# Linear attention and MoE on one core: first pair of q among k's last steps, written order from k's last quarter on

## The chip, the cores and the metric

The kernel runs on one core of a Trainium2 chip. The metric is the device time of one execution in microseconds (us); lower is better. The engines are TensorE (PE; its weight loads are PEld), VectorE (DVE), ScalarE (ACT), GpSimd (POOL) and SyncE (SP), which here only issues transfers (DMAs). GpSimd issues transfers of its own.

## The reference

`x` has 2048 tokens of 512 channels, all numbers are float32. First comes a layer norm and linear attention with 32 heads of 64, then a layer norm and a mixture of 8 experts of which each token takes two:

```python
h = layernorm(x)
q, k, v = relu(h @ Wq), relu(h @ Wk), h @ Wv          # (2048, 512) @ (512, 2048)
kv = einsum('hsd,hse->hde', k, v); key_sum = k.sum(tokens)
out = (q @ kv) / clip(q . key_sum, 1e-6)               # for each head
x = x + out @ Wo + bo
f = layernorm(x)
top2 = top_k(f @ gate_w.T + gate_b + bias, 2); gates = softmax(top2)
x = x + sum over the two experts: gate * (silu(f @ w1[e].T + b1[e]) @ w2[e].T + b2[e])
```

## The kernel before

**Numbers.** A float32 operand is split into a high and a low part (`split`: a cast on ScalarE, a subtraction on VectorE or GpSimd), and a product is three products of parts (`mm3`, L175 to L177). So each weight that is loaded (`raw_load` into one of four `raw` buffers) costs a cast and a subtraction (`raw_split`, L181) before TensorE can use it.

**Steps of k and g.** The inner width of 2048 is worked in four quarters `j` of 512, the tokens in 16 tiles `t` of 128. A step is `s = 16 j + t`; there are 64. `a_step(s)` loads what the next step needs, splits weights that fall due, multiplies the tile with Wk (`a_k`: products `pk`, then relu on ScalarE at L298, low part and running sum on VectorE at L299 and L307), and multiplies the normed tokens of step `s - 1` with that step's k (`a_g`: four banks `g`, summed over the quarter). Because v is linear in the tokens, kv follows from g and Wv once a quarter: `a_kv(j - 1)` at the third step of the next quarter, with the key sums `pks` (L355). In the first quarter each step also normalises and transposes a tile (`a_norm`), and writes it to DRAM (`xnd`), from where later quarters load it (`a_xn`).

**Work laid beside the steps.** w1 of the experts is split and written back to DRAM in 22 pieces, one a step from step 16 to 37 (one staging buffer, `stage`). k's next weights are loaded at `t == 8` and split at 9 to 12, v's loaded at 12 and split at 13 and 14. GpSimd fills rows of `out` and of the routed tokens `xs_d` with zeros (31 and 7 transfers, early in the kernel), copies part of Wq and w2 in DRAM, adds sums of token halves (`a_sums`, for the pairs below), and stores the transposed tokens to DRAM (`xtd`, in steps 32 to 47).

**Pairs of q.** The first two quarters of q are computed for pairs of token tiles with seven products instead of eight (Strassen's scheme in Winograd's form): `group(i)` for eight pairs. A group makes `p1, p6, p7, p4, p5, p2, p3` (`b_p`), adds them up on VectorE into four q's, normalises each (`normalised`, L444 to L449: five VectorE operations), and turns and multiplies the four q's of the pair before (`b_t`: four transposes, a cast, a subtraction; `b_o2`: 12 triples of products). The weights of the seven products lie where k's tokens were (`w7`), so tokens must be loaded back (`reload`, from `xtd`) for the last two quarters of q. Those run tile by tile (`b_q`, `b_n`, `b_t`, `b_o`, `b_add`), as do the routing and the experts after them.

**Wo.** `b_w(j, p)` splits a part of Wo, `b_m(j, p)` multiplies it with kv into `m_at` (`pm`), so that the output is q times m.

**What sets the order.** Outside of `with tc.manual_schedule(engines=...)` a scheduler orders each engine's instructions by its own estimate of time; inside of it, the named engines take them as written. Before, the 64 steps are ordered by the scheduler, with `hold(held, behind)` as the only order given by hand; groups are in written order on all engines but GpSimd (L1111), the steps 34 to 47 of q by the scheduler again, what follows by hand. Each engine takes its instructions in order, and so do the queues of SyncE and GpSimd.

Of the kernel before, what the change touches and what calls it, by code (L numbers as in the profile page):

```python
# [26 lines left out]
def linear_attention__then__moe_kernel(  # L27
# [207 lines left out]
    def norm(xt, dst):  # L235
        sm = const.tile([P, 16], FP, tag="sm", bufs=3, name="sm")
        st, mv, sd, rs = sm[:, 0:6], sm[:, 6:8], sm[:, 8:9], sm[:, 9:10]
        first = nc.vector.bn_stats(st, xt)
        nc.vector.bn_aggr(mv, st)
        root = nc.scalar.activation(sd, mv[:, 1:2], AF.Sqrt, bias=eps)  # L240
        nc.vector.reciprocal(rs, sd)
        last = nc.vector.tensor_scalar(dst, xt, mv[:, 0:1], rs, ALU.subtract, ALU.mult)
        return first, root, last
# [18 lines left out]
    def transpose4(src, name):  # L262
        tp = aux_bank(name)
        tp3 = tp.rearrange("p (c s) -> p c s", c=4)
        for c in range(4):
            nc.tensor.transpose(tp3[:, c, :], src[:, ts(c, P)], ident)  # L266
        return tp3
# [4 lines left out]
    def a_norm(t):  # L272
        xn = fpb.tile([P, C], FP, tag="xn", bufs=3, name="xn")
        ins = norm(xs.pop(t), xn)
# [54 lines left out]
    def a_kv(j):  # L329

        for p0 in range(0, PP, 2):
            pkv = aux_bank("pkv").rearrange("p (a l b) -> p a l b", a=2, l=2)
            for p in range(p0, p0 + 2):
                for c in range(CC):
                    w, g = slot_n[0][:, c], g_at(j)[:, c]
                    nc.tensor.matmul(
                        pkv[:, p - p0], w[:, 0, ts(p, P)], g[:, :, ts(p, P)],
                        start=c == 0, stop=False,
                    )
                    nc.tensor.matmul(  # L340
                        pkv[:, p - p0, 0, :], w[:, 1, ts(p, P)], g[:, 0, ts(p, P)],
                        start=False, stop=c == CC - 1,
                    )
            for r in range(0, P, D):
                o = slice(r, r + D)
                kv = fpb.tile([P, 2, D], FP, tag="kvs", bufs=2, name="kvs")[o]
                nc.scalar.copy(kv, pkv[o, :, 1, o])
                nc.vector.tensor_add(kv, kv, pkv[o, :, 0, o])
                split(kvt[o, 0, p0 : p0 + 2, o], kvt[o, 1, p0 : p0 + 2, o], kv)
        words(nc.sync, kvd[j], kvt)  # L350
        pks = aux_bank("pks")
        ka = frw.tile([P, 2, QW], FR, tag="xs", bufs=3, name="ka")
        split(ka[:, 0, :], ka[:, 1, :], kacc[j])
# [87 lines left out]
    def normalised(qn, q, j):  # L441

        qk = fpb.tile([P, QW], FP, tag="kacc", bufs=2, name="qk")
# [9 lines left out]
    def b_t(s, ring=None):  # L453
        tp3 = transpose4(qs.pop(s), "qtp")
# [7 lines left out]
    def b_w(j, p):  # L462
        w = wo_at(j, p)
        raw_split(("o", j, p), w[:, 0, :], w[:, 1, :], nc.gpsimd if j == 1 else nc.vector)
# [45 lines left out]
    def b_p(i, n):  # L510

        bank = acc_bank(f"p{n}")
# [10 lines left out]
    def b_o2(t, js, part=None):  # L523

        if part != 1:
            pos[t] = (mm_bank if part is None else acc_bank)("po")
# [121 lines left out]
    for _ in range(WARM):  # L648
# [14 lines left out]
    n_w1 = W1N // 512  # L663

    q_splits = {
        4: [(1, 0), (1, 1)], 10: [(6, 0), (6, 1)], 11: [(7, 0), (7, 1)], 12: [(5, 0), (5, 1)],
        13: [(3, 0), (3, 1)], 14: [(4, 0), (4, 1)], 15: [(2, 0), (2, 1)],
    }
    g_order = [NG - 1, *range(NG - 1)]
    NC = 2  # L670
    k_done = {}

    def a_step(s):
# [11 lines left out]
        if t == 8 and j + 1 < NQ:  # L685
            for c in range(CC):
                hold([raw_load(("k", j + 1, c), wk[ts(c, P), ts(j + 1, QW)])], k_done[s - 1])
        if t in (9, 10, 11, 12) and j + 1 < NQ:
            c = t - 9
            w = slot_s[(j + 1) % 2]  # L690
            raw_split(
                ("k", j + 1, c), w[:, c, 0, :], w[:, c, 1, :], nc.vector if j else nc.gpsimd
            )
        if j == NQ - 1:
            if t == 2:
                for k in range(4):
                    hold([wq_load(k)], k_done[s - 1])
            for n, c in q_splits.get(t, ()):
                wq_split(n, c)
            if t in (8, 9):  # L700
                wq_sums(t - 8)
        if t == 12:
            for c in range(CC):
                raw_load(("v", j, c), wv[ts(c, P), ts(j, QW)])
        if t in (13, 14):
            for c in (2 * t - 26, 2 * t - 25):
                raw_split(
                    ("v", j, c), slot_n[0][:, c, 0, :], slot_n[0][:, c, 1, :],
                    nc.vector if j else nc.gpsimd,
                )  # L710

        w = s - NT
        if 0 <= w < n_w1:
            if w == 0:
                hold([raw_load(("w1", 0), w1[:, ts(0, 512)])], k_done[s - 1])
# [3 lines left out]
            if w + 1 < n_w1:  # L719
                hold([raw_load(("w1", w + 1), w1[:, ts(w + 1, 512)])], k_done[s - 1])  # L720
        k_done[s] = a_k(s)
        if s:
            a_g(s - 1)
        if j and t == 2:
            a_kv(j - 1)

        if j in (1, 2) and t in (3, 5, 7, 9):
            hold([a_sums(4 * (j - 1) + (t - 3) // 2)], k_done[s])
        if s == NT:
            hold([nc.gpsimd.dma_start(wqd.bitcast(FP), wq[:, 0 : 2 * QW])], k_done[s])  # L730
        if j == 2:
            ins = nc.gpsimd.dma_start(xtd[t].bitcast(FP), xT[t].bitcast(FP))
            hold([ins], k_done[s])
        if j == NQ - 1:

            if t == 2:
# [3 lines left out]
            if 3 <= t < 3 + PP:  # L740
                b_w(0, t - 3)
                b_m(0, t - 3)
            if t == NT - 1:
# [73 lines left out]

    zero = temp()
    pool.memset(zero[:, 0 : C + 1], 0.0)
    pool.memset(zero[:, C + 1 : C + 2], -1.0)  # L820
    for b in range(NT + NZ):
        pool.dma_start(out[S + b * P : S + (b + 1) * P, :], zero[:, 0:C])
    for b in range(SPARE):
        pool.tensor_scalar(zero[:, C + 2 : CX], part, float(2 * S + b * P), None, ALU.add)
        pool.dma_start(xs_b[NB + b], zero)
    for e in range(E2):
        pool.dma_start(w2d[e, 0:HF].bitcast(FP), w2[e])
        pool.dma_start(w2d[e, HF : HF + 1].bitcast(FP), b2[e : e + 1, :])
# [24 lines left out]
    for s in range(NC, NQ * NT):  # L853
        a_step(s)
    a_g(NQ * NT - 1)
# [142 lines left out]
    def c_gate(i0, i1):  # L998
# [10 lines left out]
    NS = NQ * NT  # L1009
    engines = {  # L1010
        mybir.EngineType.PE, mybir.EngineType.DVE, mybir.EngineType.Activation,
        mybir.EngineType.SP,
    }

    def group(i):

        t0 = 2 * g_order[i]
        prev = [2 * g_order[i - 1] + n for n in range(2)] if i else []

        def place(tag):  # L1020
            return fpb.tile([P, CP if tag == "x" else C], FP, tag=tag, bufs=3, name="q")[:, 0:QW]

        def reload(*tiles):
            for t in tiles if i == NG - 1 else ():
                words(nc.sync, xT[t], xtd[t])

        add = nc.vector.tensor_add
        p1 = b_p(i, 1)
        reload(0, 1)
        q11 = place("xn")  # L1030
        b_fill(4 * i, nc.scalar.copy(q11, p1))
        p6 = b_p(i, 6)
        reload(2, 3)
        q12 = place("x")
        add(q12, q11, p6)
        turn(i - 1, 0)
        p7 = b_p(i, 7)
        reload(4, 5)
        q22 = place("xn")
        add(q22, q12, p7)  # L1040
        turn(i - 1, 1)
        if i == 0:
            a_kv(NQ - 1)
            load_tiles(1)
        p4 = b_p(i, 4)
        q21 = place("x")
        add(q21, q22, p4)
        turn(i - 1, 2)
        if i == 1:
            b_w(1, 1)  # L1050
            b_m(1, 0)
        p5 = b_p(i, 5)
        reload(6, 7)
        add(q22, q22, p5)
        b_fill(4 * i + 1, add(q12, q12, p5))
        turn(i - 1, 3)
        if i == 1:
            b_w(1, 2)
            b_m(1, 1)
        p2 = b_p(i, 2)  # L1060
        add(q11, q11, p2)
        if i == 1:
            b_w(1, 3)
            b_m(1, 2)
        p3 = b_p(i, 3)
        normalised(q21, q21, 0)
        b_fill(4 * i + 2, add(q12, q12, p3))
        qs.update({(t0, 0): q11, (t0, 1): q12, (t0 + 1, 0): q21, (t0 + 1, 1): q22})
        if i == 1:
            b_m(1, 3)  # L1070
# [11 lines left out]
        if i == NG - 1:  # L1082
            b_kv(2)
            for p in range(PP):
                load_o(2, p)
        if i == 0:
            b_w(1, 0)
        normalised(q22, q22, 1)
        if prev:
            b_o2(prev[0], (0, 1))  # L1090
        normalised(q11, q11, 0)
        if prev:
            b_put(prev[0])
            b_o2(prev[1], (0, 1))
        b_fill(4 * i + 3, normalised(q12, q12, 1))
        if prev:
            b_put(prev[1])

    def turn(i, n):

        if i >= 0:
            t, j = ((0, 0), (0, 1), (1, 1), (1, 0))[n]
            b_t((2 * g_order[i] + t, j), "kk" if n == 3 else None)

    def b_put(t):
        x1 = x1s.pop(t)
        nc.vector.tensor_add(x1, x1, pos.pop(t))
        nc.sync.dma_start(x1d[t], x1)


    with tc.manual_schedule(engines=engines):  # L1111
        load_sums(1)
        for p in range(PP):
            load_o(1, p)
        b_kv(1)
        for i in range(NG):
# [7 lines left out]
        for n in range(4):  # L1124
            turn(NG - 1, n)
# [3 lines left out]
        for t in last:  # L1129
            b_o2(t, (1, 0), 0)  # L1130
        b_q(s + 1)
        for t in last:
# [385 lines left out]
```

## Time and profile before

Three runs took 1043.14, 1040.37 and 1036.57 us, median 1040.37.

| The profiled execution | |
|---|---|
| time | 1043.51 us |
| span, first to last instruction | 1041.8 us |
| mean granted TensorE clock | 0.976 |
| TensorE, products | busy 990.1 us, 95% |
| VectorE | busy 599.2 us, 58% |
| ScalarE | busy 333.4 us, 32% |
| GpSimd | busy 366.5 us, 35% |
| DMA | 247.59 MB, mean 238 GB/s |

The profile's page gives totals, then the span in 40 slices of 26 us, with busy shares in tenths and the clock that TensorE was granted. The list of waits says, for a line of code on an engine, what it waited for: total, times and longest in us. The chain of waits is the chain of work that ended last, each piece with its start and length. Stages: steps of k and g to 396 us, pairs to about 590, tile by tile q to about 725, then the last quarter with the routing, the experts from about 835 on.

### The profile page before, as it was taken

How to read it: one execution, taken by the hardware profiler on the slowest of the kernel's cores; microseconds unless marked ns; L12 is line 12 of the kernel's file. 1: busy time of each engine (PE TensorE's matmuls, PEld its weight loads, DVE VectorE, ACT ScalarE, POOL GpSimd, SP SyncE). 2: the span in 40 equal slices, each digit the busy share in tenths (PEclk: the TensorE clock that was granted, in tenths of full speed). 3: DMA queues.
4: the chain of work that ended last, by engine and by line, in shares of the span. 5: the costliest groups of instructions: out<-in, count | busy, mean ns of one | idle time of the engine just before them, and what ended most of it. 6: DMA issues, size and time to landing. Idle time of an engine off the chain costs nothing.

```text
span 1041.8 us, 14986 instructions
## 1 busy us (share of the span) xinstructions
PE 990.1 (95%) x4854; PEld 823.4 (79%) x4854; DVE 599.2 (58%) x1422; ACT 333.4 (32%) x659; POOL 366.5 (35%) x474
## 2 busy tenths in 40 slices
PE   8999998999999998699999997999999999999994
PEld 5878876888888887488888785888888889889983
DVE  7863435353446434688888855576777768223331
ACT  4333322231134312211111222132444557444441
POOL 3643278018614002534344322131232220643354
PEclk9999998999999999799999998999999999999997
DMA  6984788878977344679995999568766498875788
GB/s 228 388 319 165 267 291 291 332 267 313 338 244 270 98 161 136 239 219 287 287 324 182 378 309 291 193 210 299 243 213 200 150 313 272 152 128 103 128 148 130
DMA packets 92667, 247.59 MB, mean 238 GB/s; under 512 B 11928, under 2 KB 15288, under 8 KB 90496
## 3 DMA queue, kind: packets, MB, share of 16 engines
q1 hardware_dynamic: 62784, 145.56, 42.1%
q0 software_dynamic: 29808, 101.07, 32.9%
q8 instruction: 42, 0.69, 0.3%
q14 instruction: 33, 0.27, 0.1%
HBM read 128.89 MB, written 126.15 MB: 245 GB/s over the span
## 4 chain that ended last, share of the span: by engine, by line
PE 76%; DMA 12%; DVE 6%; ACT 2%; issue 2%; POOL 1%; SPq 1%; POOLq 0%; ACTq 0%; DVEq 0%
PE po L175 5%; PE po L176 5%; PE po L177 5%; PE g L176 4%; PE g L177 4%; PE g L175 4%; PE pk L177 4%; PE pk L175 4%; PE pk L176 4%; DMA raw<-in_wq 3%; PE p L175 2%; PE p L177 2%; PE p L176 2%; PE py L175 2%; PE py L177 2%; PE py L176 2%
## 5 line engine op out<-in xcount | busy, mean ns | idle before, releaser
L641 POOL DMA_DIRECT2D xs_d<-temp x136 | 73.4, 546 | 133.1 <-ACT q L429 60.1
L175 PE MATMUL po<-area,qT 128*128 128x512 f32 x256 | 102.9, 402 | 7.0 <-ACT qT L181 7.0
L176 PE MATMUL g<-k,xn_hl 128*128 128x512 f32 x256 | 101.6, 397 | 2.6 <-DVE k L299 2.5
L175 PE MATMUL pk<-area 128*128 128x512 f32 x256 | 102.1, 399 | 2.0 <-ACT area L181 2.0
L177 PE MATMUL pk<-area 128*128 128x512 f32 x256 | 100.9, 395 | 0.9 <-DVE area L181 0.8
L176 PE MATMUL po<-area,qT 128*128 128x512 f32 x256 | 101.2, 395 | 0.0
L177 PE MATMUL g<-k,xn_hl 128*128 128x512 f32 x256 | 100.8, 394 | 0.0
L177 PE MATMUL po<-area,qT 128*128 128x512 f32 x256 | 100.5, 393 | 0.0
L181 DVE TENSOR_TENSOR area<-raw,area 128x512 fp32r<-128x512 f32 x65 | 53.4, 837 | 81.7 <-ACT area L181 65.0
L176 PE MATMUL pk<-area 128*128 128x512 f32 x256 | 99.9, 390 | 0.0
L1407 POOL DMA_INDIRECT out<-ys,dest x37 | 58.3, 1576 | 110.0 <-ACT ys L1404 103.1
L175 PE MATMUL g<-k,xn_hl 128*128 128x512 f32 x256 | 88.9, 396 | 2.5 <-ACT k L298 2.5
L181 ACT CAST area<-raw 128x512 fp32r<-128x512 f32 x78 | 47.4, 621 | 112.6 <-DMA raw<-in_w 34.7
L299 DVE SCALAR_TENSOR_TENSOR k<-pk,k 128x512 fp32r<-128x512 f32 x64 | 43.8, 684 | 64.7 <-ACT k L298 64.6
L181 ACT CAST qT<-qtp 128x512 fp32r<-128x512 f32 x64 | 37.4, 587 | 127.7 <-PE qtp L266 127.7
L298 ACT ACTIVATE k<-pk 128x512 fp32r<-128x512 f32 x64 | 38.1, 596 | 86.9 <-PE pk L177 86.8
L175 PEld LDWEIGHTS po<-area,qT 128*128 128x128 f32 x256 | 48.5, 189 | 18.0 <-ACT qT L181 7.8
L176 PEld LDWEIGHTS g<-k,xn_hl 128*128 128x128 f32 x256 | 48.6, 190 | 14.7 <-DVE k L299 4.3
L175 PEld LDWEIGHTS g<-k,xn_hl 128*128 128x128 f32 x256 | 47.8, 189 | 14.1 <-ACT k L298 4.2
L177 PEld LDWEIGHTS pk<-area 128*128 128x128 f32 x256 | 48.2, 188 | 12.9 <-DVE area L181 1.7
L175 PEld LDWEIGHTS pk<-area 128*128 128x128 f32 x256 | 48.3, 189 | 12.2 <-ACT area L181 2.5
L616 POOL DMA_INDIRECT xs_d<-xn,place x32 | 31.2, 974 | 75.5 <-ACT qT L181 50.2
(266 smaller groups left out, 2388.7 us busy)
## 6 DMA issues: line engine op xcount, KB each, us to landing
xs_d<-temp POOLq DMA_DIRECT2D x143, 257.5 KB, 6.5
xn_hl<-xnd SPq DMA_DIRECT2D x48, 512.0 KB, 4.6
area<-xtd SPq DMA_DIRECT2D x30, 512.0 KB, 8.2
w1d<-area SPq DMA_DIRECT2D x44, 256.0 KB, 2.4
area<-w1d POOLq DMA_DIRECT2D x16, 704.0 KB, 7.0
xg<-xs_d SPq DMA_DIRECT2D x37, 257.5 KB, 3.6
xnd<-xn_hl SPq DMA_DIRECT2D x16, 512.0 KB, 3.7
sd<-area POOLq DMA_DIRECT2D x8, 1024.0 KB, 7.9
```

What stands on the lines that cost most here:

```text
L175: first = nc.tensor.matmul(o, lh, rh, start=start, stop=False)
L176: nc.tensor.matmul(o, lh, rl, start=False, stop=False)
L177: nc.tensor.matmul(o, ll, rh, start=False, stop=stop)
L181: return nc.scalar.copy(hi, src), on.tensor_sub(lo, src, hi.bitcast(FP))
L298: relu = nc.scalar.activation(k[:, 0, :], pk, AF.Relu)
L299: nc.vector.scalar_tensor_tensor(k[:, 1, :], pk, 0.0, k[:, 0, :].bitcast(FP), ALU.max, ALU.subtract)
L616: ins = nc.gpsimd.indirect_dma_start(xs_d[:, :], at_place(t, n), xn2, None)
L641: hold([nc.gpsimd.dma_start(xs_b[e * SB + n], rows)], behind)
L1407: added[i] = nc.gpsimd.indirect_dma_start(out[:, :], bass.IndirectOffsetOnAxis(dest[:, i : i + 1].bitcast(U32), 0), ys, None, compute_op=A ...
```

## The change

1. The first pair's products `p1, p6, p7, p4, p5` are made in steps 60 to 63 (`first_pair`), in other banks; `p2`, `p3`, kv of the last quarter, turns and the first half of the outputs follow in `first_end`. The group that comes next makes the second half. Groups 1 to 7 are as before but for small shifts.
2. Steps 48 to 63 and all groups are in written order, now with GpSimd too. So are steps 34 to 47 of q.
3. Tokens are reloaded two tiles at a time, each held behind an instruction, from the last group on to step 36 of q, instead of eight and eight at once.
4. w1's 22 pieces go to steps 15, 18 to 25, 34 to 41, 48 to 50, 54 and 55; k's and v's weights and the sums move between them. The low parts of k's and v's first weights go from GpSimd to VectorE.
5. The zero fills and copies of w2 leave the start: one a step, from step 19 to 59 (`a_later`: 31 and 7 fills, then the three copies).
6. From the seventh tile on, the first norm's last operation is on ScalarE.
7. Token stores move to steps 44 to 59, the key sums' products to `t == 6`, Wq's load to `t == 1`.

The diff, cut to what matters:

```diff
-    def norm(xt, dst):
+    def norm(xt, dst, on_scalar):
...
-        last = nc.vector.tensor_scalar(dst, xt, mv[:, 0:1], rs, ALU.subtract, ALU.mult)
+        if on_scalar:
+            nc.vector.scalar_tensor_tensor(nr, mv[:, 0:1], -1.0, rs, ALU.mult, ALU.mult)
+            last = nc.scalar.activation(dst, xt, AF.Identity, bias=nr, scale=rs)
...
-        ins = norm(xs.pop(t), xn)
+        ins = norm(xs.pop(t), xn, t > 5)
...
+    w1_steps = [
+        NT - 1, *range(NT + 2, NT + 10), *range(2 * NT + 2, 2 * NT + 10),
+        *range(3 * NT, 3 * NT + 3), 3 * NT + 6, 3 * NT + 7,
+    ]
+    v_steps = {}
+    for j in range(NQ):
+        for c in range(CC):
+            s = 11 + c if j == 0 else 14 + c if j + 1 < NQ else 14 + c // 2
+            v_steps.setdefault(j * NT + s, []).append((j, c))
+    sum_steps = [NT + 4, NT + 6, NT + 8, *range(2 * NT + 3, 2 * NT + 12, 2)]
+    XT0 = 3 * NT - 4
+    q_splits = {4: [1], 5: [6], 8: [7], 9: [5], 11: [3], 12: [4], 14: [2]}
+    MAN = (NQ - 1) * NT
+    FIRST = NQ * NT - 4
...
-        if t == 8 and j + 1 < NQ:
+        t_k = 10 if j else 6
+        if t == t_k - (2 if j else 1) and j + 1 < NQ:
...
-        if t in (9, 10, 11, 12) and j + 1 < NQ:
+        if t_k <= t < t_k + CC and j + 1 < NQ:
...
-            raw_split(
-                ("k", j + 1, c), w[:, c, 0, :], w[:, c, 1, :], nc.vector if j else nc.gpsimd
-            )
+            raw_split(("k", j + 1, c), w[:, c, 0, :], w[:, c, 1, :])
...
+        if s in w1_steps:
+            w = w1_steps.index(s)
             raw_split(("w1", w), stage[:, 0, :], stage[:, 1, :])
             for l in range(2):
                 words(nc.sync, w1d[l][:, ts(w, 512)], stage[:, l, :])
+        if s + 1 in w1_steps:
+            w = w1_steps.index(s + 1)
+            hold([raw_load(("w1", w), w1[:, ts(w, 512)])], k_done[s - 1])
         k_done[s] = a_k(s)
+        if s >= FIRST:
+            first_pair(s)
         if s:
             a_g(s - 1)
         if j and t == 2:
             a_kv(j - 1)
+        if j and t == 6:
+            a_ka(j - 1)
+            a_ks(j - 1)
...
+    def a_later(s):
+        n = s - FIRST + len(later)
+        if 0 <= n < len(later):
+            job, *of = later[n]
+            hold(job(*of), k_done[s])
...
+    def first_pair(s):
+        f = first
+        if s == FIRST:
+            p1 = b_p(0, 1, aux_bank)
+            f["q11"] = spot("xn")
+            b_fill(0, nc.scalar.copy(f["q11"], p1))
+        elif s == FIRST + 1:
+            p6 = b_p(0, 6, aux_bank)
...
+            add(f["q12"], f["q11"], p6)
+        elif s == FIRST + 2:
+            p7 = b_p(0, 7, aux_bank)
...
+            add(f["q22"], f["q12"], p7)
+            p4 = b_p(0, 4, aux_bank)
...
+            b_fill(1, add(f["q21"], f["q22"], p4))
+            for n in range(2):
+                b_x1(2 * g_order[0] + n)
+        elif s == FIRST + 3:
+            p5 = b_p(0, 5, aux_bank)
+            add(f["q22"], f["q22"], p5)
+            add(f["q12"], f["q12"], p5)
...
+            normalised(f["q21"], f["q21"], 0, f["qk"])
+            load_sums(1)
+            for p in range(PP - 1):
+                load_o(1, p)
+
+    def first_end():
+        f = first
+        t = 2 * g_order[0]
+        p2 = b_p(0, 2, mm_bank)
+        add(f["q11"], f["q11"], p2)
+        p3 = b_p(0, 3, mm_bank)
+        b_fill(2, add(f["q12"], f["q12"], p3))
...
+        normalised(f["q11"], f["q11"], 0, f["qk"])
+        pkvs = [kv_products(NQ - 1, p0) for p0 in range(0, PP, 2)]
+        b_kv(1)
+        load_tiles(1)
+        for n in (1, 0):
+            b_t((t + n, 0), bank=acc_bank)
+        b_w(1, 0)
+        for p0 in range(0, PP, 2):
+            kv_out(NQ - 1, p0, pkvs[p0 // 2])
+        words(nc.sync, kvd[NQ - 1], kvt)
+        a_ka(NQ - 1)
+        load_sums(2)
+        load_tiles(2)
+        b_o2(t, (0, 1), 0)
+        normalised(f["q22"], f["q22"], 1, f["qk"])
+        b_o2(t + 1, (0, 1), 0)
+        b_fill(3, normalised(f["q12"], f["q12"], 1, f["qk"]))
+        load_o(1, PP - 1)
...
+    def reload(t, behind):
+        for n in range(2):
+            ins = nc.sync.dma_start(xT[t + n].bitcast(FP), xtd[t + n].bitcast(FP))
+            hold([ins], behind)
...
-    with tc.manual_schedule(engines=engines):
...
+    with tc.manual_schedule(engines=engines | {mybir.EngineType.Pool}):
+        for s in range(MAN, NQ * NT):
+            a_step(s)
+            a_later(s)
+        a_g(NQ * NT - 1)
+        first_end()
+        for i in range(1, NG):
             group(i)
...
-        for t in range(NT // 2, NT):
-            words(nc.sync, xT[t], xtd[t])
...
+    ordered.enter_context(tc.manual_schedule(engines=engines))
     for s in range(2 * NT + 2, NS - NT):
...
+        if t in (2, 3, 4):
+            reload(2 * t + 6, q_done[s])
         if t == 4:
             for c in range(CC):
                 raw_load(("q", j + 1, c), wq[ts(c, P), ts(j + 1, QW)])
-        if t in (5, 6, 7, 8):
-            c = t - 5
+        if 6 <= t < 6 + CC:
+            c = t - 6
...
```

## The prediction

> **What bounds the kernel now.** I read the page first: engine totals, then the 40 slices.
>
> ```profile
> PE 990.1 (95%) x4854; PEld 823.4 (79%) x4854; DVE 599.2 (58%) x1422; ACT 333.4 (32%) x659; POOL 366.5 (35%) x474
> PE   8999998999999998699999997999999999999994
> PEclk9999998999999999799999998999999999999997
> DMA  6984788878977344679995999568766498875788
> ```
>
> TensorE is busy 95%, and the change removes none of its products. It can only win back what TensorE loses by idling and by a lower granted clock. PE and PEclk dip together in three places: slice 7 (about 160 us), slices 16 and 17 (about 430) and slice 25 (about 640). The list of TensorE's waits gives the causes.
>
> ```profile
> PE po L175 <- ACT qT L181: 7.0, 1, 7.0
> PE qtp L266 <- DVE q L449: 6.8, 1, 6.8
> PE pm L176 <- POOL area L181: 2.8, 1, 2.8
> PE pks L355 <- ACT ka L181: 2.7, 1, 2.7
> PE g L176 <- DVE k L299: 2.5, 1, 2.5
> PE g L175 <- ACT k L298: 2.5, 4, 0.8
> ```
>
> The table of narrow stretches shows what the clock adds (after the busy columns: granted clock, DMA share, GB/s).
>
> ```profile
> 166.10:172.90 6.80, 5.94 (x14) 4.74 (x15) 3.89 (x7) 1.11 (x2) 3.32 (x4) 0.50 0.86 313
> 408.40:411.80 3.40, 3.40 (x10) 2.63 (x9) 0.69 (x1) 0.80 (x2) 1.28 (x1) 0.50 0.97 317
> 424.60:428.90 4.30, 4.27 (x15) 3.61 (x15) 4.02 (x8) 0.58 (x1) 0.00 (x0) 0.50 1.04 322
> 436.60:442.60 6.00, 6.00 (x14) 4.75 (x15) 1.66 (x3) 1.69 (x3) 3.51 (x5) 0.50 0.31 113
> 642.00:647.40 5.40, 5.40 (x13) 4.24 (x14) 5.40 (x12) 3.05 (x6) 1.99 (x4) 0.50 0.72 226
> ```
>
> After each long wait TensorE runs at half clock for some microseconds; half of such a stretch is lost. The loss within reach:
> - **Start:** gaps of 0.9 and 0.8 us near 68 us, for k's second weights: 1.7.
> - **Near 129:** 0.7, and a pm product at 326 that starts 1.0 late.
> - **Steps 19 to 25:** gaps of 0.7, 0.8 and 2.5 (157 to 167) and half of 6.8: 7.4.
> - **End of the k steps and first pair (396 to 443):** idle 0.2, 2.7, 6.8, 2.8, and half of 3.4, 4.3 and 6.0: 19.3.
> - **End of the pairs (590 to 648):** idle 1.0 and 7.0, and half of 5.4: 10.7.
>
> Together 40.8 us. The rest (start-up, routing, experts, tail) is not touched. The chain of waits says what was late in each place:
>
> ```profile
> 150.85 4.99 DMA raw<-in_w
> 155.94 0.63 ACT area L181
> 156.59 0.69 DVE area L181
> 158.50 5.41 DMA raw<-in_wk
> 164.07 2.23 DVE area L181 x2
> 416.53 13.72 DMA x<-in_x
> 619.49 21.31 DMA raw<-in_wq
> ```
>
> At 150 to 166 ScalarE and VectorE, whose queues run in order, sit on w1's load and then on k's weights, loaded one step before their split; the relu of k stands behind them. At 416 GpSimd waits for x, with the split of Wo behind it. At 619 Wq's next quarter stands behind eight tokens of reloads.
>
> **The change part by part.** The step of k and g is 5.49 us (relus at 369.05 and 374.50; 24 products, 0.229 each).
>
> *Norm on ScalarE for ten tokens; zero fills out of the start.* VectorE loses 10 x 0.63 (row xn<-xt) and gains 10 small operations of about 0.16 (row of the reciprocal); ScalarE gains 10 x 0.82 (row xn<-x,sm). VectorE is busy 66.9 of the first 101 us, ScalarE 38.7, so both fit. The 38 fills and three weight copies (12 MB) leave a start where DMA ran at 377 GB/s, share 0.98, and where k's weights took 10.8 us to land. They now start one step ahead of their split in a lighter queue. VectorE takes their four subtractions from GpSimd, 4 x 0.69, inside its idle time. Ends 0 and 1.7; I take all of it: the start loses 0.
>
> *w1 in pieces at steps 18 to 25 and 34 to 41, k's weights loaded two steps ahead.* The last cause at 158 (k's weights) goes. The w1 chain stays: load 4.0 to 5.0, casts 0.63 and 0.71, issue 0.5, so 5.7 to 6.1 us a piece against a step of 5.49. Beside it now stand one fill a step, the 2 MB copy of Wq at step 19 and sums at 20, 22 and 24. Bytes of steps 18 to 25: xn 4.2, w1 6.3, fills 1.8, sums 3.1, Wq 2.1, kv and k's weights 1.6: 19.1 MB in 48 us (eight steps and 4.1 for kv), 398 GB/s. At 377 that is 2.7 us late, at 333 (570 to 642 us) 9.4. I take 3.0, near the first, since 7 MB of it have no reader in these steps. The second batch asks 18.4 MB, 383 GB/s: 0.8 to 7 late; I take 1.0, since before's 34 to 37 had the same pieces beside the token stores without a gap. "DMA: Bandwidth & Descriptors" of the Trainium skill, Specifications, gives 358 GB/s of HBM for a core, and its section on issuing engines says that GpSimd's and SyncE's transfers share the same engines; by these the first term would be an estimated 5.3 instead of 3.0, though the trace moves 377.
>
> *First pair among steps 60 to 63.* Five of seven products (30 x 0.229 = 6.9 us) move from behind the steps to between them: no TensorE time by itself. VectorE has eight operations of 0.69 (5.5 us) in step 62, and six and a normalisation (6.6) in step 63, against 8.2 and 6.9 of TensorE, so it keeps up; without that cover each further one would cost 0.69. The loads that come along (x for two tokens, sums of the next pair, three parts of Wo: 2.4 MB) and six fills fall where DMA moves 128 GB/s at a share of 0.38 (347 to 396); so do the token stores, now at steps 44 to 59. What is won is VectorE's start. Count from the last g product. VectorE: splits of g to 1.7 (397.87 against 396.1), additions to 3.6, one normalisation of 2.5 (rows 0.60, 0.72, 0.24, 0.24, 0.69) to 6.1. TensorE: p2 and p3 2.75, kv 3.65 (400.35 to 404.0), two turns 1.0: 7.4. The turned q needs a cast and a subtraction, ready at 8.3: idle 0.9. Two half outputs (24 products) to 13.8, p1 and p6 of the next pair to 16.6. VectorE meanwhile: turned q to 8.9, Wo 0.6, four kv pieces of 0.96 each to 13.3, key sum 0.9, two normalisations 5.0: 19.2. So the turn of q12 waits 2.6 us. Before, a wait of 2.7 was followed by 3.4 us at half clock, so 1.7 more. Into the second pair 0.8, since its outputs are half as long (5.5 against 11 us). Sum 6.0. Ends: 0, and 12 if VectorE is as late as it was at 424. "TensorE: Matmul & The Clock Gate" of the Trainium skill, section "Why this matters for your kernels", holds that only gaps above about 3 us drop the clock; by that the sum would be 4.3, but this trace drops it after 2.7.
>
> *GpSimd in written order.* Its split of Wo stands ahead of the additions to x, so the 2.8 us wait at 436 goes. Ahead of it stay three fills of 0.54 each. Behind a late fill, Wo's split and then pm would be late, up to 2.8 again (inside the 12).
>
> *Step order from 48 on.* Wq is loaded at step 49 (2 MB), with w1's next piece behind it. ScalarE reaches that piece ahead of the relu of step 50; g(50) comes some 17 us after the load's issue (5.5 + 5.5 + 3.65 + 2.75), so 8 us of queue are covered. The key sums' two products go from step 2 of a quarter to step 6, away from the 0.7 at 129, which I leave with the 1.0 as they are (ends 0 and 1.7). From 650 to 725 the order was the scheduler's, with TensorE busy 76.99 of 77; by hand it is 0 to 2, I take 1.0.
>
> *Reloads by pairs.* The stretch 570 to 642 moved 23.95 MB in 72 us, share 0.99. The bytes stay; without its losses it has 61.3 us, which asks 391 GB/s. At 377 it ends 2.2 late, at 333 10.6, which is nothing won. What changes is who waits: Wq now has two steps of some 6 us before its split and not eight tokens ahead but two. I take 4.0.
>
> **Sum.** Left: 0 + 0.7 + 3.0 + 1.0 + 1.0 + 6.0 + 4.0 + 1.0 = 16.7. Won: 40.8 - 16.7 = 24.1. The profiled execution took 1043.5 us (span 1041.8), so 1019.4. It lies 3.1 above the median of its three runs, 1040.4, from which the sum would give 1016.3; I say **1018**.
>
> **Rivals.**
> - *Clean:* all waits go: 1043.5 - 40.8 = 1002.7. For it: VectorE is 58% busy. Against it: its order behind the last g product, and 377 to 398 GB/s asked for. Chance 0.12.
> - *Transfers keep the waits:* pairs' end 10.7 and steps 19 to 25 7.4 as before, first pair 10, the others 3.7: left 31.8, so 1034.5. For it: share 0.99 at 570 to 642. Against: the waits hung on two loads placed badly. Chance 0.15.
> - *Slower: the w1 chain.* Sixteen pieces, one a step, with fills, sums and stores beside them. A piece takes its load plus 1.85; covered are 5.49 a step and 8.2 in all (kv twice). The other edits are worth 28 (24.1 and the chain's own 4), so it decides at 16 x (load + 1.85 - 5.49) - 8.2 = 28, a load of 5.9 us. At 7.0 us it costs 45.6: 1043.5 - 28.1 + 45.6 = 1061. For it: a load of the same size took 10.8 us at 55 us and one of x 13.7. Against: 3.3 to 5.0 at 133 to 156 us. Chance 0.10.
> - *Forecast,* 1008 to 1030: chance 0.63.
>
> **Numbers.** Runs of before spread by 6.6 us, so about 1% (10 us) is what can be told from no change: faster means below 1030. Faster is forecast, clean and a little of the second rival: 0.77; within 1% 0.13; slower 0.10. The range runs from the clean case to the second rival's upper side, 1003 to 1038: about 0.10 + 0.63 + 0.11.
>
> **What would show it.** Right: slices near 430 and 640 at 9 in PE and PEclk; DMA in slice 1 below 9; no x<-in_x or raw<-in_wq piece over 10 us in the chain; a wait of about 2.6 us of a turn for VectorE's normalisation near the end of k. Wrong: waits of g for ScalarE or VectorE between steps 18 and 41, with long raw<-in_w pieces; or po waiting for turned q after the pairs.

## The result, and the profile after

Twenty runs of the changed kernel have a median of 1049.95 us (1040.88 to 1055.21), twenty of the kernel before 1042.57 us (1034.33 to 1048.07). The ratio is 1.0075, interval 1.0053 to 1.0097: some 8 us slower, not 24 faster. The profiled execution took 1051.67 us, its span is 1049.9.

The page's totals of the changed kernel, and its slices (26 us each, tenths of busy time):

```profile
PE 992.1 (94%) x4854; PEld 822.9 (78%) x4854; DVE 618.5 (59%) x1431; ACT 341.3 (33%) x669; POOL 355.7 (34%) x465
...
PE   8999997999978999889999999899999999999994
...
PEclk9999999999999899999999999899999999999997
DMA  6633688678979796768896987879766498876788
```

The dip near 430 us is smaller (slices 17 and 18 at 8; before 16 and 17 at 8 and 6). But slices 12 and 13 (289 to 341 us), at 9 before, are at 7 and 8, slice 7 (about 165) went from 8 to 7, and slice 26 is at 8 where 25 was at 7. TensorE's list of waits names them (total, times, longest in us):

```profile
PE g L175 <- DVE area L181: 6.9, 1, 6.9
PE g L175 <- DMA xn_hl<-xnd: 6.4, 2, 5.5
PE qtp L270 <- DVE q L467: 5.3, 3, 2.7
PE pm L175 <- DMA area<-kvd: 4.1, 1, 4.1
PE po L177 <- DVE qT L181: 2.7, 1, 2.7
```

The waits of 7.0 (po) and 6.8 (qtp) of before are gone, with smaller ones of up to 2.7 us in their place. Three that were not there stand in k's steps: 5.5 us at 164, 6.9 at 312 and 4.1 at 342. The table of narrow stretches shows TensorE at half clock around each and after the pairs (after the busy columns: granted clock, DMA share, GB/s):

```profile
163.70:167.10 3.40, 2.95 (x7) 2.40 (x8) 2.25 (x3) 0.43 (x1) 3.40 (x5) 0.50 1.04 405
310.40:317.30 6.90, 5.06 (x12) 3.99 (x13) 4.99 (x9) 3.34 (x7) 1.12 (x3) 0.51 0.91 306
341.20:348.00 6.80, 6.18 (x15) 4.87 (x16) 6.06 (x6) 1.69 (x3) 6.62 (x6) 0.50 0.78 315
665.40:672.30 6.90, 5.93 (x16) 4.76 (x17) 4.55 (x9) 0.41 (x1) 0.49 (x1) 0.51 0.95 328
```

The chain of waits says what was late (start, length, what):

```profile
132.11 10.97 DMA raw<-in_w
...
147.73 3.91 DVE area L181
151.65 5.91 DMA w1d<-area
...
158.78 5.23 DMA xn_hl<-xnd
...
299.87 4.09 DMA sd<-area
...
310.78 4.96 DMA raw<-in_w
...
334.10 7.59 DMA area<-kvd
...
642.94 8.68 DMA x1d<-x
651.64 0.32 SPq L438
...
652.98 8.22 DMA raw<-in_wq
```

- **164:** a piece of w1 takes 11.0 us to load beside the 2 MB copy of Wq, its split 3.9 and its store 5.9. SyncE's queue then stands behind a load of k's weights that needs a buffer, and the normed tokens (`xn_hl`) behind that.
- **312:** a store of the sums (`sd`), the last but one, lands at 304.0, 9.6 us behind step 47's relu; before, the last of them landed 2.7 us behind it. ScalarE, in written order from step 48, has the split of v next, into the same staging region. It idles 9.1 us, with the relu of k and three pieces of w1 behind it.
- **342:** the load of kv stands behind what came late.
- **666:** a load of x1 keeps SyncE's queue until a store of x1 has landed, 8.7 us; the reloads and Wq's last quarter are behind it.

Gaps and half of the half-clock stretches, summed by place, against before: k's steps behind the start 27.3 us (9.1), first pair 9.7 (19.3), end of the pairs 9.8 (10.7); the start's 1.7 are gone. Together 46.8 against 40.8, 6.0 of the 8.1 us by which the spans differ.

### The profile page after: what moved, and what is told of

Same layout as the page of the kernel before. It is cut to its first block, busy times and chain, and to the rows that moved or that the text cites. A ratio compares the mean times of both kernels' runs of the same rounds, so it can differ in the third digit from the quotient of the medians.

```text
span 1049.9 us, 14980 instructions
## 1 busy us (share of the span) xinstructions
PE 992.1 (94%) x4854; PEld 822.9 (78%) x4854; DVE 618.5 (59%) x1431; ACT 341.3 (33%) x669; POOL 355.7 (34%) x465
## 4 chain that ended last, share of the span: by engine, by line
PE 77%; DMA 12%; DVE 6%; ACT 2%; issue 2%; POOL 1%; SPq 1%; POOLq 0%; ACTq 0%; DVEq 0%
PE po L175 5%; PE po L177 5%; PE po L176 5%; PE pk L175 4%; PE g L175 4%; PE pk L177 4%; PE g L176 4%; PE pk L176 4%; PE g L177 4%; DMA raw<-in_w 3%; PE qtp L270 3%; PE pq L175 2%; PE p L177 2%; PE p L175 2%; PE p L176 2%; PE py L175 2%
## 5 line engine op out<-in xcount | busy, mean ns | idle before, releaser
L181 DVE TENSOR_TENSOR area<-raw,area 128x512 fp32r<-128x512 f32 x74 | 67.6, 926 | 98.3 <-ACT area L181 93.3
L175 PE MATMUL g<-k,xn_hl 128*128 128x512 f32 x256 | 95.8, 400 | 14.3 <-DVE area L181 6.9
L176 PE MATMUL g<-k,xn_hl 128*128 128x512 f32 x256 | 101.5, 397 | 1.4 <-DVE k L303 1.4
L177 PE MATMUL g<-k,xn_hl 128*128 128x512 f32 x256 | 101.1, 395 | 0.0
L462 DVE SCALAR_TENSOR_TENSOR qk<-q,ksb 128x512 f32<-128x512 f32 x64 | 46.2, 722 | 26.7 <-ACT q L446 26.7
L177 PEld LDWEIGHTS po<-area,qT 128*128 128x128 f32 x256 | 48.6, 190 | 14.9 <-DVE qT L181 4.1
L175 PEld LDWEIGHTS po<-area,qT 128*128 128x128 f32 x256 | 48.5, 189 | 13.1 <-ACT qT L181 2.9
L175 PEld LDWEIGHTS pk<-area 128*128 128x128 f32 x256 | 48.7, 190 | 12.2 <-ACT area L181 1.4
```

The source lines that it names most:

```text
L175: first = nc.tensor.matmul(o, lh, rh, start=start, stop=False)
L176: nc.tensor.matmul(o, lh, rl, start=False, stop=False)
L177: nc.tensor.matmul(o, ll, rh, start=False, stop=stop)
L181: return nc.scalar.copy(hi, src), on.tensor_sub(lo, src, hi.bitcast(FP))
L462: nc.vector.scalar_tensor_tensor(qk, q, 0.0, ksb[j], ALU.max, ALU.mult)
```

## The experiments

The ratios are to the kernel before, with their intervals; "after" is the changed kernel (1.0075). Microseconds below or above after are differences of these ratios; their intervals make most of them uncertain by 3 to 5 us, e7's by 8. Gaps are read from one profiled execution of each kernel. GpSimd's queue takes its DMA issues and its arithmetic in one order. In after a zero fill stands in it once a step from step 19 on, behind that step's relu of k, between the pieces of the sums. GpSimd's own list of waits in after has, for these fills (`out`):

```profile
POOL out L879 <- ACT k L302: 36.0, 11, 5.2
```

From step 44 on the token store of the step stands right in front of the fill and waits for the same relu.

**First set: one place each.** All start from after.

```diff
 e2  -    sum_steps = [NT + 4, NT + 6, NT + 8, *range(2 * NT + 3, 2 * NT + 12, 2)]
     +    sum_steps = [*range(NT + 4, NT + 11, 2), *range(2 * NT + 3, 2 * NT + 10, 2)]
 e3  -        if s == NT + 3:      # copy of Wq in DRAM
     +        if s == 9:
 e4  -            if t == 1:       # loads of Wq, steps from 48
     +            if t == 0:
     and b_kv(0) ahead of the four loads of Wo
 e6  e2, e3 and e4 together
```

> The changed kernel with one list altered: the eight sums of token halves start at steps 20, 22, 24, 26, 35, 37, 39 and 41, none at 43. Placement theory: the wait of 6.9 us of g near 312 us hangs on the last sums, whose store ends after the split of v's weights falls due in written order at step 48; with the half clock behind it (2.5) it goes, so 9.4 us less than the changed kernel, about 1040.5. Fills theory (the zero fills laid beside the steps slow every transfer): the fills stay, so no more than 2 us are won. Written-order theory (any load that is late blocks ScalarE now): the wait moves to w1's next load in the same steps, at most 4 us are won.

Measured: 1.0075 (1.0044 to 1.0105). The gap at 312 fell to 2.7, but ScalarE waited as long at v's split (9.2 us, 9.1 in after): the store it needs, here the sums' last, landed 9.7 us behind step 47's relu, and the gap of pm grew to 5.7. Written two steps sooner, the last sums do not free the region sooner.

> The changed kernel with the 2 MB copy of Wq in DRAM started at step 9 instead of 19, where DMA moves 138 GB/s (75 to 100 us). Placement theory: the copy stretched a load of w1 to 11.0 us near 132 us, and the wait of 5.5 us of g near 164 with 1.5 of half clock goes: 7 us less, about 1043. Fills theory: won is less than 2 us, because the fills, sums and w1's stores still fill DMA from 125 to 175 us.

Measured: 1.0049 (1.0027 to 1.0071). The gap at 164 fell from 5.5 to 1.8 without half clock, as said; 2.8 us of gaps came at 250, and 4.7 of pm at 688. The ratio is 2.6 thousandths below after's, which is not clear of the noise.

> The changed kernel with the 2 MB load of Wq at step 48 instead of 49 and the load of kv ahead of Wo's four loads at step 50. Placement theory: the wait of 4.1 us of pm for kv near 342 us and the half clock behind it (3.1) go: 7 us less, about 1043; w1's pieces of steps 49 and 50 may pay 1 to 3 of it, since Wq's load is now beside the first of them. Fills theory: less than 2 us won. Written-order theory: ScalarE waits for w1's piece behind Wq instead, 0 to 3 us won.

Measured: 1.0108 (1.0068 to 1.0147). pm waits as long (4.3 us near 342), now for ScalarE's split and not for kv; the theory on the order of these loads fell.

> The changed kernel with all three: sums from step 20 to 41, Wq's copy at step 9, Wq's load at step 48 with kv first. Placement theory: the three add up, 9.4 + 7 + 7 = 23 us less than the changed kernel, about 1027, faster than before by 1.5%. Fills theory: within 6 us of the changed kernel. If the waits only move on to the next late transfer, between 1035 and 1045.

Measured: 1.0039 (1.0016 to 1.0062), 3.8 us below after. The waits moved: gaps at 160, at 250 to 277, 307, 326 and 339. That three loads placed badly cost 23 us is thereby refuted; what makes them late has to lie further upstream.

**Second set: what is upstream.** e1 puts fills and copies of w2 back at the start, e5 begins the written order at step 60, e7 puts the token stores (`xtd`) back at steps 32 to 47, e8 is e1 with e7.

```diff
 e1  -    def a_later(s): ...      # one fill a step, held behind k_done[s]
     +    for job, *of in later:
     +        hold(job(*of), k_done[NC - 1])
 e5  -    MAN = (NQ - 1) * NT
     +    MAN = NQ * NT - 4
 e7  -    XT0 = 3 * NT - 4
     +    XT0 = 2 * NT
```

> The changed kernel with the 38 zero fills and the three copies of w2 issued in one go early, as before, instead of one a step. GpSimd-queue theory (the held fills and token stores of GpSimd's queue make the sums late and fill DMA in steps 48 to 54): the wait near 312 falls from 6.9 to under 3, the one near 342 from 4.1 to 1 to 2, half clocks with them; the start pays back its 1.7. Net 5 to 9 us less than the changed kernel, 1041 to 1045. Written-order theory (ScalarE waits in the order in which the text has the splits, whatever GpSimd does): the waits near 312 and 342 stay within 2 us, net 0 to 3 us more, 1050 to 1053.

Measured: 0.9950 (0.9920 to 0.9980), 13 us below after and below before. No gap at 164 nor at 250 to 278; the sums' last store lands at 296.8. The start pays: 3.6 us of gaps and 1.7 of half clock near 55 us. (The profiled execution is the fastest of the ten, 1032.3 us against a median of 1038.7.)

> The changed kernel with steps 48 to 59 left to the scheduler; written order starts at step 60. Written-order theory: ScalarE and VectorE no longer sit on a split whose load is late ahead of the relu; the waits near 312 (6.9 + 2.5) and 342 (4.1 + 3.1) fall below 2 us together: 12 to 15 us less than the changed kernel, about 1036. GpSimd-queue theory: the loads and the sums are just as late, so the waits move but stay: 0 to 5 us less, 1045 to 1050.

Measured: 0.9977 (0.9942 to 1.0013), 10 us below after. Here the sums' last store lands at 329.5, later than ever, and nothing waits for it: no gap at 312 or 342, only 1.6 us at 317 for a load of tokens. In these two runs the late sums cost only where the written order has put v's split in front of the relu. The edit leaves the order of all engines in steps 48 to 59 to the scheduler, GpSimd's too; that it was ScalarE's order is read from its 9.1 us in after, and not tested by itself.

> The changed kernel with the 16 token stores (0.5 MB each) at steps 32 to 47, as before, instead of 44 to 59. GpSimd-queue theory: DMA of GpSimd's queue from 300 to 400 us falls from some 140 to 50 GB/s, and the load of kv (7.6 us) and w1's pieces behind Wq's load (12.1) shorten: the wait near 342 goes (7 us with its half clock); the sums of steps 35 to 43 get one more held transfer a step and come later, the wait near 312 stays or grows by 2. Net 3 to 7 us less than the changed kernel. Written-order theory: within 2 us of the changed kernel.

Measured: 1.0122 (1.0052 to 1.0192). The stores now stand among the sums, whose last store lands at 323.3, and the wait at v's split almost doubles:

```profile
PE g L175 <- DVE area L181: 12.9, 1, 12.9
```

> The changed kernel with both the fills and w2 copies at the start and the token stores at steps 32 to 47, so that GpSimd's queue moves nothing in steps 48 to 59, as before the change. GpSimd-queue theory: the waits near 312 and 342 go with their half clocks (16.6 us), the start pays 1.7: about 1035. Written-order theory: no more than 4 us less than the changed kernel, 1046 to 1050.

Measured: 1.0051 (1.0021 to 1.0081). Taking the fills out of the queue is undone by putting the stores in.

**Third set: queue or bytes.** e13 leaves every transfer of the 31 fills where it is in the steps and lets ScalarE's queue issue it; the scheduler's order of the steps before 48 changes in places with it. e12 is the kernel before with after's fills. e10 is e1 with e5.

```diff
 e13 -        return [nc.gpsimd.dma_start(out[S + b * P : S + (b + 1) * P, :], zero[:, 0:C])]
     +        return [nc.scalar.dma_start(out[S + b * P : S + (b + 1) * P, :], zero[:, 0:C])]
```

> After, with the 31 zero fills of out issued by ScalarE's queue in place of GpSimd's, at the same steps, behind the same relu; the 7 spare rows and 3 copies stay on GpSimd. Bytes and times of the transfers are as in after. Theory A (it is the held fill in GpSimd's in-order queue that costs): the sums' last store lands by step 47 and most of the 12.9 us come back, 1037 to 1042 us. Theory B (it is the fills' traffic beside w1, xn and k's weights): as after, 1047 to 1052 us.

Measured: 0.9990 (0.9962 to 1.0017), 8.9 us below after, with the same bytes. No gap at 164; the sums' last store lands at 296.7 instead of behind 304. Left in k's steps are 4.1 us of gaps at 245 to 261 and these two, which stand where the order is written:

```profile
PE pm L175 <- DMA area<-kvd: 4.1, 1, 4.1
...
PE g L175 <- DVE area L181: 2.5, 1, 2.5
```

Counted as above, k's steps lose 14.9 us here, 27.3 in after and 6.3 in e1 (which also takes the spare rows and the copies of w2 out of them). So more than half of the fills' cost is not their bytes but their place in GpSimd's queue and what it does to the order of the rest; these two were not separated, nor the 0.56 us that GpSimd takes to issue a fill from the time it waits for the relu. In the stretch of 125 to 165 us e13 moves more bytes than after (346 GB/s against 294).

> The kernel before, with only the fills and copies of w2 moved to one a step from step 19, each held behind that step's k, as after does. Theory A (a fill held in GpSimd's queue holds up the sums and with them loads and splits): the start gains about 1.5 to 5 us, the k steps lose 8 to 15: 1045 to 1055 us, slower than before. Theory B (fills cost only their bytes; the loss after is from the written order and the moved pieces): the start's gain stays, 1036 to 1041 us.

Measured: 1.0002 (0.9969 to 1.0034). The start gains 2.2 us (step 16's relu at 104.4 instead of 106.6); gaps of 2.1 at 117, 1.4 at 156 and 5.5 at 174 take it back. The sums' store lands at 318.3, and in the scheduler's order nothing waits for it. (The profiled execution, the slowest of the twelve, also has a gap of 5.7 us at 620.) Theory A's 8 to 15 us were too many here: in the kernel before, the same fills cost no more than the start gains.

> After, with the 38 fills and the weight copies back at the start and the written order beginning at step 60 instead of 48. Theory A (two separate causes: fills held in GpSimd's queue from step 19, 12.9 us of span; written order from step 48, 10 us with some of it the same waits at 301 to 342): the two add in part, the gaps at 164, 250 to 278, 301 to 343 are all gone, the start pays its 5 us; 1026 to 1033 us, below both single edits. Theory B (one cause seen twice: both edits only take ScalarE and VectorE off the late sums): no better than either alone, 1037 to 1041 us.

Measured: 0.9870 (0.9827 to 0.9912), 1030.8 us: below both kernels. The two causes nearly add (12.5 and 9.8 thousandths alone, 20.5 together).

**Fourth set: without the price at the start, and the other two places.** e15 is e13 with e5; e14 is e15 with q22 normalised ahead of kv's pieces; e16 is after with the token stores on ScalarE's queue.

> After, with the 31 fills of out on ScalarE's queue and the written order from step 60. Theory (two causes, each measured alone: 8 to 9 us for the fills' queue, 10 us for the written order, partly the same waits at 301 to 342, and no price at the start): no gap at 164, 302 and 331, step 48's relu by 294, span 1024 to 1031. Rival (the waits at 302 and 331 stay whatever the order, since the late sums were only one cause): as with the fills on ScalarE's queue alone, 1040 us or more.

Measured: 0.9883 (0.9848 to 0.9918). Step 48's relu comes at 294.9 (309.6 in after); no gap at 164 or 302; 2.2 us at 323 are left. The four kernels after, e13, e5 and e15 have each combination of the two edits: the fills' queue is worth 8.5 thousandths in written order and 9.4 without it, the order 9.8 and 10.7. In the kernel before, the fills cost nothing on balance (e12), so their cost in GpSimd's queue comes together with something else of the change, such as the moved sums and pieces of w1; what it is was not tested.

> After, with only the 16 token stores of steps 44 to 59 issued by ScalarE's queue; the fills stay on GpSimd. Theory A (every held transfer in GpSimd's queue costs): the gaps at 312 and 342 shrink, the one at 164 stays (no token store stands there), 2 to 5 us less than after. Theory B (the fills alone fill that queue): as after, within 1.5 us.

Measured: 1.0112 (1.0074 to 1.0150). Nothing is gained. But GpSimd's queue is held as before: in steps 44 to 47 it now idles 1.4 to 2.4 us in front of the fill, which waits for the same relu as the store did. The run does not tell whether the stores alone would cost.

> As the kernel with ScalarE's fills and written order from 60, and in the first pair's end VectorE normalises q22 ahead of kv's four pieces and the key sums instead of behind them. Theory (the turn waits for that normalisation because it stands last on VectorE, as the prediction counted): the gap of 2.4 at the turn and the half-clock stretch behind it go, 2 to 4 us less than the same kernel without this edit. Rival (kv's pieces come later and m's products wait instead): a pm wait of 1 to 3 us takes its place, no difference.

Measured: 0.9880 (0.9839 to 0.9920); the gap stays, 2.44 us against 2.43. The turn waits for q12, and moving q22 leaves all of VectorE's work ahead of q12 as it was: the edit missed its target. e18 normalises q12 first:

```diff
     b_w(1, 0)
+    b_fill(3, normalised(f["q12"], f["q12"], 1, f["qk"]))
     for p0 in range(0, PP, 2):
         kv_out(NQ - 1, p0, pkvs[p0 // 2])
```

> As the kernel with ScalarE's fills and written order from 60, with q12 (the one that is turned first in the next pair) normalised ahead of kv's four pieces and the key sums on VectorE. Theory (the turn waits for VectorE to come to that normalisation): the gap of 2.4 at the turn goes; m's products, which need kv, may wait up to 1 us; 1 to 4 us less. Rival (VectorE as a whole is late there, whatever its order): a gap of 2 us or more stays within 10 us of that place and the time is the same.

Measured: 0.9878 (0.9831 to 0.9925). The gap falls to 0.6, as the theory has it, with 1.1 of pks and pm and a stretch at half clock behind it, and the 4.1 us at the second pair's turn stay. Gaps and half clock of the first pair together are 10.7 us as in e15, and the time is the same. No gap of 2 us stays within 10 us of the place, so the rival's sign did not come either; that VectorE as a whole is late there fits, but is not shown.

**The end of the pairs.** e11 is e10 with Wq's last quarter loaded one step of q earlier; e17 is e15 with that and kv's load two steps earlier; e19 is e18 with x1 loaded three steps ahead of its use instead of four.

```diff
 e11, e17  -        if t == 4:          # and ahead of b_x1
           +        if t == 3:
                        for c in range(CC):
                            raw_load(("q", j + 1, c), wq[ts(c, P), ts(j + 1, QW)])
 e19       -        b_x1(s + 2)
           +        b_x1(s + 1)
```

> The kernel with fills at the start and written order from step 60, and Wq's last quarter loaded one step of q earlier, ahead of the load of x1 in SyncE's queue. Theory A (at the end of the pairs po waits for the split of Wq, whose load stands behind x1's load, which waits for a store): the gaps at 650 to 672 and the half-clock stretch behind them go, 3 to 5 us less than the same kernel without this edit. Theory B (the transfers there are full, so the wait only moves): within 1.5 us of it.

Measured: 0.9879 (0.9842 to 0.9915), as e10. The gaps of po at 643 to 646 went; pm waited 9.0 us for kv at 667 in their place.

> As the kernel with ScalarE's fills and written order from 60, and Wq's last quarter loaded one step of q earlier and kv of the last quarter two steps earlier, ahead of Wo's loads in SyncE's queue. Theory A (the wait at the end of the pairs is that of a load standing behind a load of x1 that waits for its store): po's gaps at 642 to 646 and pm's at 667 both go, 4 to 6 us less than the same kernel without these edits. Theory B (the transfers there are full): a third load becomes late and the time is the same.

Measured: 0.9870 (0.9836 to 0.9904), as e15. Now Wo's load is the late one. Its chain shows why each load that is moved leaves another behind: SyncE's queue stands twice for a store of x1.

```profile
657.14 5.59 DMA x1d<-x
662.74 0.32 SPq L438
663.15 3.98 DMA x1d<-x
667.15 0.32 SPq L438
667.56 2.80 DMA raw<-in_wo
```

x1 has four buffers. Loaded four steps ahead, tile s + 2 takes the buffer of tile s - 2, whose store was issued a moment ago.

> As the run with q12 first, and in the steps of q tile by tile x1 is loaded three steps ahead of its use instead of four, so that its buffer (one of four) was emptied by a store one step earlier. Theory A (each load of x1 holds SyncE's queue for the 8 us that the store just issued takes, with reloads, Wq and Wo behind it): no load of x1 waits over 2 us, po's gaps of 642 to 650 and pm's near 670 both go, 3 to 6 us less than with q12 first alone. Theory B (the transfers are full): the loads land as late, gaps as before, within 1.5 us.

Measured: 0.9792 (0.9749 to 0.9836), 1023.8 us (1022.0 to 1026.9), 9 us below e18 and the fastest of all. One sign of theory A did not come: loads of x1 still wait, up to 8.8 us. But between 600 and 672 us these waits fall from 46.1 us to 10.5, and the gaps of po and pm there are gone. The list of SyncE's waits (total, times, longest) for e18, then for e19:

```profile
SPq L438 <- DMA x1d<-x: 85.3, 19, 9.3
```

```profile
SPq L438 <- DMA x1d<-x: 30.9, 8, 8.8
```

And the slices of e19, in which the dips near 160, 310 and 640 us are gone:

```profile
PE   8999999999999999989999999999999999999994
...
PEclk9999999999999999999999999999999999999997
```

From 640 to 672 us TensorE is busy 32.0 us of 32 in e19, 28.0 in e18, while DMA moves more (282 against 266 GB/s). The transfers were not full; the queue was blocked.

## Why the prediction was wrong, point by point

| place | left, predicted | left in after | left in e19 |
|---|---|---|---|
| start (near 68 us) | 0 | 0 | 0 |
| k's steps from 129 on | 5.7 | 27.3 | 7.7 |
| first pair | 6.0 | 9.7 | 10.2 |
| end of the pairs, written order | 5.0 | 9.8 | 3.8 |
| sum | 16.7 | 46.8 | 21.7 |

- **The step that failed first: "zero fills out of the start".** The prediction booked the 1.7 us that the start gains and the fills' 1.8 MB among the bytes of steps 18 to 25, and nothing for where they wait. Each is held behind a relu in the queue that adds the sums. e13, with the same bytes at the same steps from ScalarE's queue, wins back 8.9 us. (In the kernel before the same move costs nothing on balance, as e12 shows, so the price comes with the rest of the change.) The prediction asked what stands behind a late fill only at the first pair, and counted the sums' stores as bytes; they also free the region that v's split needs, and at step 48 that split waited 9.1 us for one.
- **The second: "Step order from 48 on", priced at nothing** beside the 0.7 and 1.0 that it left as they were. The prediction asked only whether w1's next piece comes late behind Wq's load (8 us of queue). e4 moved that load and won nothing. What a written order does is fix who stands behind whom when something else is late: ScalarE waited 9.1 us at v's split with k's relu behind it. e5 wins back 10 us though the sums are later still.
- **The third: "Reloads by pairs", priced by bytes** (391 GB/s asked for, 377 to be had: 2.2 us late, 4.0 taken). From 570 to 645 us of after DMA moved 254 GB/s, at a share of 0.76. The loss is SyncE's queue standing for x1's buffer: term and written order together measured 9.8 us, and 3.8 in e19. SyncE's own list of waits in the kernel before had this wait, 46.7 us in 15 times of a load of x1 for a store of x1, and the prediction says nothing of it. 13 of the 15 stand behind 659 us, where TensorE of before loses nothing; the change lays reloads and Wq's load behind such waits. e19's edit was not run on the kernel before, so how much it would win there is not known.
- **Steps 19 to 25** (3.0 by 398 GB/s against 377): the bytes can be moved. After loses 7.0 us at 164, e15 only 0.45 at 175, so the term was no worse than it said, and the reason for after's loss was another.
- **First pair:** mechanism right. VectorE's waits came where they were said, the turn's at 2.41 us against 2.6. The mis-sized term is "into the second pair 0.8": it measured 4.5 in after (2.9 idle, 1.6 of half clock), since VectorE was as late a pair further on. Normalising q12 first won nothing (e18).
- **Start:** right. The two gaps near 68 us are gone. Step 16's relu comes at 105.0 instead of 106.6, but says little by itself: with the same start it came at 104.0 in e4 and at 106.6 in e2.
- **Rivals.** "Transfers keep the waits" had the right places and the wrong reason. The slower rival, w1 loads of over 5.9 us on average, had the right victims (ScalarE and VectorE at a late piece), but e15 has the same 16 pieces and loses 6.4 us in all of k's steps, where before lost 9.1; the pieces were not the cause. (By the prediction's own figures a piece takes 5.8 to 6.8 us, not 5.7 to 6.1; and the two relus that it gives for a step's 5.49 us are 5.45 apart, though their neighbours at 352.53 and 358.02 are 5.49.) A rival for a queue held by its own transfers was missing.
- **Signs of being wrong:** two came, the wait of g at 164 behind w1's load of 11.0 us (for tokens, not for ScalarE or VectorE), and po waiting for a turned q after the pairs (2.7 us at 666).

With the three blocked places undone, the change comes near its sum: 40.8 - 21.7 = 19.1 us won of the 24.1, and a span of 1023.2 against 1041.8. Part of this may be e19's edit itself, which the kernel before might gain from too.

## What to carry to other kernels

A transfer that is held behind another engine's work can cost its queue more than its bytes: before moving one, list what stands behind it on that queue and who reads that, and read SyncE's and GpSimd's own lists of waits as well as TensorE's. When an edit takes a wait away and another of the same size appears next to it, as in e6, e11 and e17, stop moving loads and look for what blocks the queue; at the end of the pairs it was a ring of four buffers asked for one step too early. An order written out by hand is only as good as the times it assumes: leave it to a scheduler until the late producer in front of it is cured.

## What the runs showed of the hardware

**VectorE's subtraction beside GpSimd.** The low part of a weight takes VectorE 0.69 us, and up to 4.8 where GpSimd adds sums at the same time. The mean over 74 of them is 926 ns in after and 755 in e13; the first chain above holds one of 3.9 us. In the groups of costliest instructions of after, beside k's low part, of which one operand is not a weight buffer but `pk` (the matmul's result):

```profile
L181 DVE TENSOR_TENSOR area<-raw,area 128x512 fp32r<-128x512 f32 x74 | 67.6, 926 | 98.3 <-ACT area L181 93.3
...
L303 DVE SCALAR_TENSOR_TENSOR k<-pk,k 128x512 fp32r<-128x512 f32 x64 | 44.0, 687 | 95.1 <-ACT k L302 95.0
```

Of the 74 in after, the 56 that had no GpSimd arithmetic beside them took at most 0.70 us, the 18 that had some 0.68 to 4.8. The second form was never stretched: 16 of the 64 ran beside GpSimd arithmetic and none took over 0.69. The Trainium skill's page "SBUF — State Buffer", section "Who interferes with whom", says that a VectorE instruction with both inputs in SBUF contends with a GpSimd instruction that reads SBUF, and that one with at most one such input, outside the 2-port performance modes, does not; these two rows agree with it. No run took GpSimd's work away to test it.

**The clock.** Half clock followed idle times of 2.4 us in after (at 439) and did not follow one of 2.4 at the same place in e15. In e6, at 160, it followed one of 1.7. In after it lasted about 3.4 or 6.8 us each time.
